# Four gated cross-attention layers: the stacks of score operands copied within SBUF, a shorter lead of the first pass, and the next layer's keys made during routing

## The chip, the core and the metric

The kernel runs on one core of a Trainium2 chip. A core has five engines with an instruction stream of their own: TensorE (PE; its weight loads are listed as PEld), VectorE (DVE), ScalarE (ACT), GpSimd (POOL) and SyncE (SP). They share SBUF (128 partitions) and pass matmul results through PSUM banks. Transfers between DRAM and SBUF, and within SBUF, are issued by an engine's queue and run on 16 DMA engines.

The metric is the device time of one execution in microseconds. Four runs of the kernel before gave 1860.47, 1851.73, 1857.73 and 1854.29 us, median 1856.01.

## The reference

There are 8 batch elements of 256 tokens and 256 features, a context of the same shape, and four layers. Each layer adds a gated cross-attention and a gated feed-forward part:

```python
x = x + tanh(g_xattn[l]) * xattn_l(layernorm(x), ctx)   # 16 heads of 16 features
x = x + tanh(g_ffn[l])   * ffn_l(layernorm(x))
# xattn: q = (x Wq + bq)/4, k = ctx Wk + bk, v = ctx Wv + bv;  softmax(q k^T) v Wo + bo
```

- Layer 0's attention has no projections (query and context are used as they are) and a mask over the keys. Its feed-forward part is a light and a heavy two-layer gelu network. All 256 tokens are routed to the heavy one.
- The feed-forward parts of layers 1 and 2 are mixtures of 8 experts. Each token takes the best two by its logits, weighted by a softmax over the two. The hidden widths are 1024 and 512.
- The feed-forward part of layer 3 quantizes activations and weights (to three values), convolves along the sequence over three tokens and applies silu.

## The kernel before

**Stages.** `attention(layers)` builds a region: (0, 1), then (2,), then (3,). The first region also carries layer 0's feed-forward part and the logits for layer 1's experts, the second the logits for layer 2's, the third the last feed-forward part (`pieces`). Between the regions stand `moe(...)`: `route` (best two experts), `slots` (a place for each token in 39 tiles of 128 rows, NTL = 39, by the matmuls rank L832 and tot L834 and a long row of VectorE operations behind them), and `experts`, which goes over the tiles: gather a tile's tokens, turn them (xgT L1000), hidden layer (hg L1020), output (ysb L1033), store to DRAM (yd L1034).

**A region's order.** `run` counts steps u, one per head and element (16 heads, so 128 steps per layer). At step u it emits `scores(u + LAG)` with LAG = 17, `probs(u)`, the values of an earlier head, and then whatever `plan` has put at that step. So the engines' order is written out by hand, and matmuls are pinned to it; other instructions may be moved by the scheduler within their dependences.

- `scores` makes the scores of one head (sc, L173) for its row maxima alone; VectorE reduces them (nm, L437, or with the mask ms, L432).
- `parts` and `rows` cut the negated maxima in three bf16 pieces, turn them and copy them (mt L463, then a DMA) into rows 112 to 114 of the query stack, once per half of an element (8 heads).
- `probs` makes the transposed scores again (st, L173), now with those three rows against rows of ones in the key stack, and ScalarE takes the exponential straight from PSUM (pT, L481).
- `values` multiplies by va, and `finish` projects and adds.

**The stacks.** Scores need more than one bf16 product. `split` cuts a float32 operand in three bf16 pieces with four operations (L182 to L185), and `stack` (from L240) puts pieces side by side along the contraction: seven groups of 16 partitions, the query's pieces in the order QP = (0, 1, 0, 1, 2, 0, 1), the key's in the order KP = (0, 1, 1, 0, 0, 2, 2). A stack has 16 partitions per group, and in each partition 8 heads x 512 columns. The source has its 128 partitions as (16 features, 8 heads), so partitions are regrouped on the way. Before, this goes over DRAM: one DMA writes the three pieces (dr, L248, 384 KB), then DMAs of whole rows of 8 KB read them back into the stack (L256), three for a query (neighbouring groups in one) and six for a key. SP issues them all. An element thus costs two splits, two writes and nine reads. The split of element 0 of a region runs on VectorE, the others on POOL.

```python
rows = dr.rearrange("i (d h) n -> (i d) (h n)", h=HC)
nc.sync.dma_start(st[k * DK : e * DK], rows[part[k] * DK : (part[e - 1] + 1) * DK])
```

The key stacks of elements 0 and 1 and of their values are kept outside the region (kkeep, vkeep, EARLY = 2). Their rows 96 and up are set to one by VectorE (L198).

**Preparation of an element** (`prep`): begin, `norm` (`stats` with the pow on POOL, L152, then xn L334, then x + gb on POOL, L339), `normT` (turn by TensorE, copy xs, L354/L356), `proj` of q (two halves oc = 0, 1: pq L173, then ScalarE's qT L375/L379), `proj` of k (kT L375/L381) and `vals` (va L393). Steps are counted from 16 (j - 2) - 3 for element j.

**What stands at a region's start.** Keys and values of elements 0 and 1 of the coming layer (`early`), with `setup` (weights and the product for gb), are made by `experts` at its last tiles: `setup` at tile 27, k and v of element 0 at tiles 32 to 35 and the others at the end. Before each element's norm the experts' results are added: `fetched` emits four gathers from yd on POOL (L950) at one step, `added` four VectorE operations (L1074) nine steps later. An element's first scores need its query stack, so at a region's start the chain is: gathers, added, statistics, pow, xn, turn, pq, qT, split, stack, score.

**The head.** The first region has x, context and mask loaded by SP (L281 to L285), the weights of the light and heavy network (L633 to L642) and the products with their gammas on POOL (L658, two of them on 128 x 1024).

Of the kernel before, what the change touches and what calls it, by code (L numbers as in the profile page):

```python
# [15 lines left out]
P = 128  # L16
# [12 lines left out]
LAG, AHEAD, VLAG = 17, 3, 1  # L29

# [6 lines left out]
def kernel(ctx: ExitStack, tc: tile.TileContext, a: dict, out: bass.AP):  # L37
# [51 lines left out]
    nc.vector.tensor_copy(identb, ident)  # L89
    nhalf = const.tile([P, 2, TPB], F32, tag="nhalf", name="nhalf")  # L90
# [44 lines left out]
    def stats(tiles, name, again=None):  # L135


        n = len(tiles)
        st = small.tile([P, TPB, 6], F32, tag="lnst", name=f"lnst_{name}")
        mv = small.tile([P, TPB, 2], F32, tag="lnmv", name=f"lnmv_{name}")  # L140
        for i, t in enumerate(tiles):
            nc.vector.bn_stats(st[:, i, :], x[t])
            nc.vector.bn_aggr(mv[:, i, :], st[:, i, :])
        k = 1 if again is None else 2
        ve = small.tile([P, 2, TPB], F32, tag="rsv", name=f"rsv_{name}")[:, :k, :n]
        nc.vector.tensor_scalar(ve[:, 0, :], mv[:, :n, 1], 1e-5, None, ALU.add)
        if again is not None:
            nc.vector.reciprocal(ve[:, 1, :], ve[:, 0, :])
            nc.vector.tensor_tensor(ve[:, 1, :], ve[:, 1, :], mv[:, :n, 1], ALU.mult)
            nc.vector.tensor_scalar(ve[:, 1, :], ve[:, 1, :], again[0], None, again[1])  # L150
        rs = small.tile([P, 2, TPB], F32, tag="rsr", name=f"rsr_{name}")[:, :k, :n]
        nc.gpsimd.tensor_tensor(rs, ve, nhalf[:, :k, :n], ALU.pow)  # L152
        return (mv, rs[:, 0, :]) if again is None else (mv, rs[:, 0, :], rs[:, 1, :])
# [42 lines left out]
    def ones_of(engine, va, ks=None):  # L196
        if ks is not None:
            engine.memset(ks[96:P], 1.0)  # L198
        engine.memset(va[:, :, :, DK : DK + 1], 1.0)
        engine.memset(va[:, :, :, DK + 1 :], 0.0)  # L200

    def attention(layers):
# [6 lines left out]
        stacks, vas = {}, []  # L209
# [28 lines left out]
        def stack(src, s, j):  # L238

            n = f"{s}{layers[0]}_{j}"  # L240
            pc = keep.tile([P, 3, DC * S], BF16, tag="pc", name=f"pc_{n}", bufs=2)
            r = keep.tile([P, DC * S], F32, tag="res", name=f"res_{n}")
            split(
                [pc[:, k] for k in range(3)], src.rearrange("p c s -> p (c s)"), r,
                nc.gpsimd if j and pool is not None else nc.vector,
            )
            dr = dram.tile([3, P, DC * S], BF16, tag=f"{s}dr", name=f"dr_{n}", bufs=2)
            nc.sync.dma_start(dr.rearrange("i p n -> p i n"), pc)  # L248
            st = stacks[s][j % 3].rearrange("r h c s -> r (h c s)")
            rows = dr.rearrange("i (d h) n -> (i d) (h n)", h=HC)  # L250
            part, k = QP if s == "q" else KP, 0
            while k < NS:
                e = k + 1
                while e < NS and part[e] == part[e - 1] + 1:
                    e += 1
                nc.sync.dma_start(  # L256
                    st[k * DK : e * DK], rows[part[k] * DK : (part[e - 1] + 1) * DK]
                )
                k = e
            return stacks[s][j % 3]  # L260

        ops = {}

        def prep(j, l, b):
# [4 lines left out]
            def begin():  # L269
                if l == 0 and j < EARLY:  # L270
                    ones_of(nc.vector, vas[j], stacks["k"][j])
                o["nm"] = pool.tile([P, 2, NH], F32, tag="nm", name=f"nm_{n}", bufs=3)

            def ones_own():

                nc.sync.dma_start(stacks["k"][j][NR : NR + 3], kkeep[0][NR : NR + 3])
                ones_of(nc.gpsimd, vas[j])

            def context():
                for i in range(2):  # L280
                    nc.sync.dma_start(x[2 * b + i], a["x"][b, i * P : (i + 1) * P, :])  # L281
                cx = pool.tile([P, 2, D], F32, tag="cx", name=f"cx_{n}", bufs=1)
                nc.sync.dma_start(cx, a["ctx_1024"][b].rearrange("(i p) d -> p i d", p=P))
                mk = pool.tile([P, 2, S], I32, tag="mk", name=f"mk_{n}", bufs=1)
                nc.sync.dma_start(  # L285
                    mk, a["mask_Bx1xSxS2_ik1"][b, 0].rearrange("(i p) k -> p i k", p=P)
                )
# [37 lines left out]

            def norm():
                xn = work.tile([P, 2, D], F32, tag="xn2", name=f"xn_{n}")
                mv, rs = stats([2 * b, 2 * b + 1], f"a{n}")
# [13 lines left out]
                o["xn"] = xn  # L342

            def normT():
# [10 lines left out]
                else:  # L355
                    nc.scalar.mul(xs, pt, 1.0 / DK**0.5)  # L356
                    o["qs"] = stack(xs, "q", j)
                o["xs"] = xs

            def proj(s, oc):  # L360
# [21 lines left out]
                if oc:  # L382
                    o[f"{s}s"] = stack(o["t"], s, j)
# [13 lines left out]
            own = [(0, ones_own)] if j == EARLY else []  # L397
            if l == 0:
                return own + [
                    (-3, begin), (-3, context), (-2, norm), (3, normT), (4, contextT), (5, biasT),  # L400
                    (6, contextV),
# [5 lines left out]
            if j < EARLY:  # L407
                early.extend([(NTL - 7 + i if j == 0 else NTL, f) for i, (_, f) in enumerate(kv)])
                kv = []
            return own + [  # L410
                (-6, begin), (-5, norm), (0, normT),
                (2, lambda: proj("q", 0)), (3, lambda: proj("q", 1)),
# [4 lines left out]
        def scores(u):  # L417
# [20 lines left out]
            if u - LAG in hold:  # L438
# [112 lines left out]

        def plan(at, f, *args):
            todo.setdefault(at, []).append(lambda: f(*args))

        for j, (l, b) in enumerate(jobs):
            if l and b == 0:
                if j:
                    plan(NH * (j - 2) - AHEAD - 6, setup, l)
                else:
                    early.append((NTL - 12, lambda l=l: setup(l)))  # L560
            for at, f in prep(j, l, b):
                plan(NH * (j - 2) - AHEAD + at, f)
            for c in range(DC):
                at = NH * j + HC * c + HC - LAG
                plan(at, parts, j, c)
                plan(at + 4, rows, j, c)
# [11 lines left out]
        def run(pool_, extra=(), ahead=()):  # L578
# [3 lines left out]
            for at, f in ahead:  # L582
                plan(at, f, pool)
                hold.add(at)
# [8 lines left out]
            for at, f in extra:  # L593
                plan(at, f)
            for u in range(min(todo), max(max(todo), NU + VLAG + 4) + 1):
                if 0 <= u + LAG < NU:
                    scores(u + LAG)
# [26 lines left out]
    def ffn0(pool):  # L624
# [5 lines left out]
        def load_weights():  # L630
            w1 = pool.tile([P, DC, NL + NHV], F32, tag="f0w1", name="f0w1", bufs=1)
            w2 = pool.tile([P, nh, D], F32, tag="f0w2", name="f0w2", bufs=1)
            nc.sync.dma_start(  # L633
                w1[:, :, :NL], a["L0_ffn_light_w1"].rearrange("(c p) h -> p c h", p=P)
            )
            nc.sync.dma_start(
                w1[:, :, NL:], a["L0_ffn_heavy_w1"].rearrange("(c p) h -> p c h", p=P)
            )
            nc.sync.dma_start(
                w2[:, 0:1, :], a["L0_ffn_light_w2"].rearrange("(c p) o -> p c o", p=P)  # L640
            )
            nc.sync.dma_start(  # L642
                w2[:, 1:, :], a["L0_ffn_heavy_w2"].rearrange("(c p) o -> p c o", p=P)
            )
# [11 lines left out]
            for c in range(DC):  # L656
                for cols, g in ((slice(0, NL), gl), (slice(NL, None), gh)):
                    nc.gpsimd.tensor_scalar(  # L658
                        w1[:, c, cols], w1[:, c, cols], g[:, c : c + 1], None, ALU.mult
                    )  # L660
            w.update(w1=w1, w2=w2, b1=b1, b2=b2[:, 0, :])
# [51 lines left out]
        return [(-LAG, load_weights)] + [q for b in range(B) for q in element(b)]  # L713
# [242 lines left out]
    def experts(l, pool, xd, chosen, rows, nh, scale, early, nsets, apart):  # L956
# [104 lines left out]
        def element(b):  # L1061
# [5 lines left out]
            def fetched(pool):  # L1067
                for k, (t, s, w) in enumerate(rows):
                    g.append(pool.tile([P, D], F32, tag="yg", name=f"yg{l}_{b}_{k}", bufs=4))
                    gather(g[k], yd[:, :], s[:, t : t + 1])  # L1070
# [8 lines left out]
            return [(at - 16, fetched), (at - 7, added)]  # L1079
# [212 lines left out]
    def moe(l, nh, nsets, apart, lg, xd, gate, early, scale=None):  # L1292
        with tc.tile_pool(name=f"c{l}", bufs=1) as pool:
            with tc.tile_pool(name=f"rt{l}", bufs=1) as tmp:
                chosen = route(pool, tmp, lg, gate, l)
                rows = slots(l, pool, tmp, chosen[0], chosen[1], nsets)
            with tc.tile_pool(name=f"f{l}", bufs=1) as tiles:
                return experts(l, tiles, xd, chosen, rows, nh, scale, early, nsets, apart)
# [13 lines left out]
    with tc.tile_pool(name="f3w", bufs=1) as home:  # L1312
        weights, pieces = ffn3(home)
        ahead = moe(2, 4, 5, False, lg[1], xd[1], tg[:, 6:7], early + weights, w["nw"])
# [90 lines left out]
```

## Time and profile before

The profile is of one execution of 1852.96 us; its span is 1851.2 us, with 27144 instructions. The runs' median is 1856.01 us.

| engine | busy us | share of the span |
|---|---|---|
| TensorE | 1430.1 | 77% |
| its weight loads | 1087.9 | 59% |
| VectorE | 926.5 | 50% |
| ScalarE | 740.2 | 40% |
| POOL | 676.0 | 37% |

The stages by the timeline of TensorE:

| from, to (us) | stage |
|---|---|
| 0 to 66.5 | head: loads, first norm, first stacks, scores up to the first st |
| 66.5 to 590 | region (0, 1) |
| 600 to 637 | routing and slots for layer 1's experts |
| 650 to 900 | layer 1's experts |
| 922 to 976 | start of region (2,) |
| 1201 to 1240 | routing and slots for layer 2's experts |
| 1250 to 1385 | layer 2's experts |
| 1390 to 1457 | start of region (3,) |
| 1457 to 1851 | region (3,) with the last feed-forward part |

How it is read: times are microseconds from the span's start. A line of a timeline has the start, the busy time, the engine, the line in the kernel, the operation, output<-inputs and how many such instructions are joined in it. In brackets stands the time in which the engine was idle before it and the work that ended this wait. "sc<-kstack,qstack" is the matmul that reads both stacks. The granted clock (PEclk) is a share of TensorE's full speed.

### The profile page before, as it was taken

How to read it: one execution, taken by the hardware profiler on the slowest of the kernel's cores; microseconds unless marked ns; L12 is line 12 of the kernel's file. 1: busy time of each engine (PE TensorE's matmuls, PEld its weight loads, DVE VectorE, ACT ScalarE, POOL GpSimd, SP SyncE). 2: the span in 40 equal slices, each digit the busy share in tenths (PEclk: the TensorE clock that was granted, in tenths of full speed). 3: DMA queues.
4: the chain of work that ended last, by engine and by line, in shares of the span. 5: the costliest groups of instructions: out<-in, count | busy, mean ns of one | idle time of the engine just before them, and what ended most of it. 6: DMA issues, size and time to landing. Idle time of an engine off the chain costs nothing. (4 is left out here: it accounts for less than half of the span.)

```text
span 1851.2 us, 27144 instructions
## 1 busy us (share of the span) xinstructions
PE 1430.1 (77%) x9856; PEld 1087.9 (59%) x9886; DVE 926.5 (50%) x2642; ACT 740.2 (40%) x1623; POOL 676.0 (37%) x807
## 2 busy tenths in 40 slices
PE   1598888989998499999947888739992676666653
PEld 1366566766665399999825565439991354444422
DVE  5655554445664411111154767453322657778777
ACT  0255444545554133333204555312330346455641
POOL 4342322332410344433154532025533435553452
PEclk9989999999998699999968999869996788888876
DMA  7653222223450423332454554153444434222000
GB/s 200 155 121 81 64 58 58 58 67 87 100 134 30 162 61 109 107 114 85 102 128 98 113 132 93 32 190 125 123 109 97 109 70 97 55 53 67 7 7 17
DMA packets 96381, 170.05 MB, mean 92 GB/s; under 512 B 26028, under 2 KB 80175, under 8 KB 85231
## 3 DMA queue, kind: packets, MB, share of 16 engines
q1 hardware_dynamic: 68114, 114.40, 25.1%
q0 software_dynamic: 23664, 52.81, 9.7%
q10 hardware_dynamic: 4470, 1.10, 0.3%
q8 instruction: 78, 1.28, 0.3%
q14 instruction: 55, 0.45, 0.1%
HBM read 224.69 MB, written 41.68 MB: 144 GB/s over the span
## 5 line engine op out<-in xcount | busy, mean ns | idle before, releaser
L481 ACT ACTIVATE pT<-st 128x512 f32<-128x512 f32 x512 | 298.3, 597 | 289.4 <-PE st L173 232.3
L437 DVE TENSOR_REDUCE nm<-sc 128x2 f32<-128x512 f32 x384 | 257.0, 684 | 150.2 <-PE sc L173 148.3
L173 PE MATMUL sc<-kstack,qstack 112*128 112x256 bf16 x1024 | 213.3, 294 | 119.1 <-DMA kstack<-dr_k 53.1
L1020 ACT ACTIVATE hg<-phg,we 128x128 f32<-128x128 f32 x468 | 133.8, 369 | 269.4 <-issue 232.5
L173 PE MATMUL phg<-xgT,we 128*128 128x128 f32 x1872 | 225.2, 277 | 9.3 <-DMA we<-in_L_ffn_w,sl_wrow 3.9
L173 PEld LDWEIGHTS phg<-xgT,we 128*128 128x128 f32 x1872 | 223.5, 194 | 14.8 <-issue 9.3
L173 PE MATMUL st<-qstack,kstack 115*128 115x256 bf16 x1024 | 206.2, 285 | 28.0 <-ACT pT L481 26.8
L173 PE MATMUL yg<-we,hg 128*128 128x256 f32 x936 | 214.6, 379 | 0.0
L173 PEld LDWEIGHTS <-qstack 112*128 112x128 bf16 x1024 | 100.7, 104 | 187.9 <-issue 109.4
L173 PEld LDWEIGHTS yg<-we,hg 128*128 128x128 f32 x936 | 171.9, 190 | 20.2
L173 PE MATMUL po<-pT,va 128*32 128x256 f32 x2048 | 149.9, 409 | 0.9
L432 DVE CUSTOM_DVE_ANT_0 ms<-sc,mb 128x256 f32<-128x256 f32 x256 | 107.6, 420 | 76.9 <-PE sc L173 66.7
L173 PEld LDWEIGHTS <-kstack 115*128 115x128 bf16 x1024 | 104.1, 102 | 55.2 <-issue 36.1
L1033 DVE TENSOR_TENSOR ysb<-yg,we 128x256 f32<-128x256 f32 x78 | 33.0, 424 | 165.2 <-PE yg L173 155.6
L950 POOL DMA_INDIRECT xg<-xd,sl_toki x78 | 76.9, 986 | 89.2 <-DVE sl_toki L946 65.9
L152 POOL TENSOR_TENSOR rsr_ff<-rsv_ff,nhalf 128x4 f32<-128x4 f32 (+2 forms) x24 | 24.4, 1017 | 226.3 <-DVE rsv_ff L150 120.3
L950 POOL DMA_INDIRECT yg<-yd,sl_si x64 | 62.6, 978 | 103.2 <-DVE x L1074 31.1
L173 PEld LDWEIGHTS po<-pT,va 128*32 128x32 f32 x2048 | 56.2, 114 | 60.8 <-issue 37.3
L1000 DVE COPY xgT<-ptg 128x256 f32<-128x256 f32 x39 | 16.6, 425 | 139.8 <-PE ptg L178 139.8
L178 PE MATMUL px<-ident,xn 128*128 128x128 f32 x128 | 26.9, 346 | 69.6 <-DVE xn L334 59.6
L182 POOL CAST pc_q<-qT 128x512 bf16<-128x512 f32 x22 | 13.8, 628 | 172.4 <-ACT qT L375 126.7
L173 PE MATMUL pq<-xs,wq 128*128 128x256 f32 x192 | 67.1, 483 | 4.4 <-ACT qT L375 1.9
(253 smaller groups left out, 2508.7 us busy)
## 6 DMA issues: line engine op xcount, KB each, us to landing
kstack<-dr_k SPq DMA_DIRECT2D x160, 128.0 KB
qstack<-dr_q SPq DMA_DIRECT2D x64, 256.0 KB
dr_q<-pc_q SPq DMA_DIRECT2D x32, 384.0 KB
dr_k<-pc_k SPq DMA_DIRECT2D x32, 384.0 KB
qstack<-dr_q SPq DMA_DIRECT2D x32, 384.0 KB
yd<-ysb SPq DMA_DIRECT2D x78, 128.0 KB
kstack<-dr_k SPq DMA_DIRECT2D x32, 256.0 KB
xd<-fxn_f SPq DMA_DIRECT2D x8, 512.0 KB
```

Source lines behind the costliest of these rows:

```text
L152: nc.gpsimd.tensor_tensor(rs, ve, nhalf[:, :k, :n], ALU.pow)
L173: pin(nc.tensor.matmul(out, lhsT=lhsT, rhs=rhs, start=start, stop=stop, skip_group_check=True))
L178: pin(nc.tensor.transpose(out, in_, idn))
L182: engine.tensor_copy(dst[0], src)
L432: nc.vector.tensor_tensor_reduce(masked, sc[:, i, :], o["bias"][:, i, :], -1.0, 3.0e38, ALU.add, ALU.min, o["nm"][:, i, h : h + 1],)
L437: nm = nc.vector.tensor_reduce(o["nm"][:, :, h], sc, AX.X, ALU.max, negate=True)
L481: pin(nc.scalar.activation(pT[u], st, AF.Exp))
L950: return nc.gpsimd.indirect_dma_start(out=dst, out_offset=None, in_=src, in_offset=bass.IndirectOffsetOnAxis(ap=rows, axis=0), **kw,)
L1000: nc.vector.tensor_copy(xT, pv)
L1020: nc.scalar.activation(h[:, hc, :], ph[:, k, :], AF.Gelu, bias=w[:, n1 - nh + hc : n1 - nh + hc + 1],)
L1033: nc.vector.tensor_tensor(ys, py, w[:, nh * D :], ALU.add)
```

## The change

1. `stack` has no way over DRAM any more. Seven DMAs of 16 partitions x 8 x 1 KB each copy a piece of the split result (pc, 128 partitions) straight into its group of the stack, ordered by piece, all on SP. 64 stacks: 448 such DMAs in place of 352.
2. In regions (2,) and (3,) element 0's query is stacked by halves: each `proj("q", oc)` is split at once (256 columns, VectorE) and copied into half c of the stack (rows of 512 B), its DMAs by turns on SP (4) and ACT (3). Element 1's query is split on VectorE, and key stacks always on POOL.
3. FIRST = 14: the first head is scored 14 steps ahead of its exponential. The lead grows by one head in two steps to 17 (`slot`). `parts` and `rows` of element 0 follow.
4. Element 1's preparation is planned 8 steps later. `stats` becomes a step of its own (`measure`), and in regions (2,) and (3,) its pow is pinned in program order for elements 0 and 1. The four gathers of an element are emitted one per step and pinned.
5. The ones rows of the key stack come by DMA from a tile of ones. The loads of the light and heavy network stand at step -4 and are pinned; the products with their gammas at steps 8 and 10, pinned on POOL. ctx is loaded ahead of x and mask in a pinned order.
6. `early` (setup, keys and values of elements 0 and 1) runs between `route` and `slots` and no longer in the last tiles of `experts`. The ternary weights of the last feed-forward part stay in `experts`.

The diff's core:

```diff
-LAG, AHEAD, VLAG = 17, 3, 1
+LAG, FIRST = 17, 14
+AHEAD, VLAG = 3, 1
...
-    def ones_of(engine, va, ks=None):
-        if ks is not None:
-            engine.memset(ks[96:P], 1.0)
+    def ones_of(engine, ks, va):
+        nc.sync.dma_start(
+            ks[NR : NR + 3].rearrange("r h c s -> r (h c s)"), onesb[: 3 * HC * DC * S // P]
+        )
...
-            dr = dram.tile([3, P, DC * S], BF16, tag=f"{s}dr", name=f"dr_{n}", bufs=2)
-            nc.sync.dma_start(dr.rearrange("i p n -> p i n"), pc)
...
+            if c is not None:
+                cols = slice(c * S, (c + 1) * S)
+                pc, r, src, st = pc[:, :, cols], r[:, cols], src[:, cols], st[:, :, c, :]
+            else:
+                st = st.rearrange("r h c s -> r h (c s)")
+            split([pc[:, k] for k in range(3)], src, r, engine or nc.gpsimd)
+            part = QP if s == "q" else KP
+            for n, (p, k) in enumerate(sorted((p, k) for k, p in enumerate(part))):
+                e = nc.scalar if c is not None and n % 2 else nc.sync
+                d = e.dma_start(st[k * DK : (k + 1) * DK], pc[:, p])
+                if layers[0] == 0 and j == 0:
+                    pin(d)
...
-                if oc:
-                    o[f"{s}s"] = stack(o["t"], s, j)
+                if s == "q" and lead and j == 0:
+                    o["qs"] = stack(o["t"], s, j, oc, nc.vector)
+                elif oc:
+                    o[f"{s}s"] = stack(
+                        o["t"], s, j, engine=nc.vector if s == "q" and lead and j == 1 else None
+                    )
...
             return own + [
-                (-6, begin), (-5, norm), (0, normT),
-                (2, lambda: proj("q", 0)), (3, lambda: proj("q", 1)),
+                (-6, begin), (-5, measure), (-3 + k, norm), (0 + k, normT),
+                (2 + k, lambda: proj("q", 0)), (3 + k, lambda: proj("q", 1)),
             ] + kv
...
+        slot = []
+        for u in range(-FIRST, NU):
+            while len(slot) < min(NU, u + 1 + min(LAG, FIRST + max(0, u // 2))):
+                slot.append(u)
...
             for c in range(DC):
-                at = NH * j + HC * c + HC - LAG
+                at = slot[NH * j + HC * c + HC - 1] + 1
                 plan(at, parts, j, c)
-                plan(at + 4, rows, j, c)
+                plan(at + (3 - (c == 0) if j == 0 else 4), rows, j, c)
...
-        return [(-LAG, load_weights)] + [q for b in range(B) for q in element(b)]
+        return [(-4, load_weights)] + [(8 + 2 * c, lambda c=c: gammas(c)) for c in range(DC)] + [
+            q for b in range(B) for q in element(b)
+        ]
...
-            return [(at - 16, fetched), (at - 7, added)]
+            return [(at - 16 + k, lambda p, k=k: fetched(p, k)) for k in range(4)] + [
+                (at - 7, added)
+            ]
...
                 chosen = route(pool, tmp, lg, gate, l)
+                for f in early:
+                    f()
                 rows = slots(l, pool, tmp, chosen[0], chosen[1], nsets)
```

In TensorE's order the early matmuls then stand behind plf (the logits of the last tokens) and ahead of tot: gb's product, k and v of element 0, k and half of v of element 1, rank, the rest of v, tot.

## The prediction

> **What bounds the kernel now.** I read the shares of the engines first.
>
> ```profile
> PE 1430.1 (77%) x9856; PEld 1087.9 (59%) x9886; DVE 926.5 (50%) x2642; ACT 740.2 (40%) x1623; POOL 676.0 (37%) x807
> ```
>
> TensorE leads, but 23% of the span it stands. Where it stands is told by windows cut at the stages' seams (the last column but two is the granted clock, then DMA share and GB/s):
>
> ```profile
> core 0: us, PE busy (x) PEld busy (x) DVE busy (x) ACT busy (x) POOL busy (x), PEclk, DMA share, GB/s
> 0.00:66.50 66.50, 14.24 (x62) 8.84 (x63) 39.07 (x133) 5.29 (x9) 25.58 (x40) 1.00 0.81 199
> 66.50:590.00 523.50, 471.25 (x3373) 333.39 (x3401) 277.49 (x1031) 273.08 (x510) 151.13 (x187) 0.96 0.34 81
> 600.00:637.00 37.00, 9.68 (x72) 8.82 (x73) 20.41 (x81) 1.82 (x4) 9.89 (x10) 0.53 0.26 97
> 650.00:900.00 250.00, 250.00 (x1715) 234.96 (x1714) 31.80 (x73) 79.05 (x276) 99.81 (x101) 1.00 0.34 103
> 922.00:976.00 54.00, 23.86 (x85) 14.41 (x84) 27.29 (x67) 5.19 (x13) 26.33 (x31) 0.66 0.49 115
> 1201.00:1240.00 39.00, 7.92 (x57) 6.85 (x56) 24.80 (x84) 0.49 (x2) 8.83 (x9) 0.51 0.38 132
> 1390.00:1456.70 66.70, 24.37 (x89) 14.72 (x88) 27.72 (x68) 5.84 (x13) 26.73 (x35) 0.62 0.41 95
> ...
> 1401.00:1403.00 2.00, 0.00 (x0) 0.00 (x0) 0.00 (x0) 0.00 (x0) 1.62 (x2) 0.50 1.01 135
> 949.50:952.50 3.00, 0.21 (x1) 0.24 (x2) 0.73 (x2) 0.00 (x0) 2.14 (x4) 0.50 1.02 254
> ```
>
> The first attention region is TensorE's (471 of 523), the experts wholly so (250 of 250). Between them lie five seams in which it idles: the head (to 66.5), two routings (600, 1201), the starts of the second and third region (922, 1390). The change works in all five. The timeline of TensorE names what ends a start's wait (in brackets: idle time before, and its releaser):
>
> ```profile
> 42.23 1.01 PE L173 MATMUL sc<-kstack,qstack 112*128 112x256 bf16 x4 [20.50 <-DMA kstack<-dr_k]
> 954.72 0.61 PE L173 MATMUL sc<-kstack,qstack 112*128 112x256 bf16 x2 [1.34 <-DMA qstack<-dr_q]
> 976.08 0.50 PE L173 MATMUL st<-qstack,kstack 115*128 115x256 bf16 x2
> 1001.61 0.58 PE L173 MATMUL sc<-kstack,qstack 112*128 112x256 bf16 x2 [6.29 <-DMA kstack<-dr_k]
> 1433.38 0.58 PE L173 MATMUL sc<-kstack,qstack 112*128 112x256 bf16 x2 [1.95 <-DMA qstack<-dr_q]
> ```
>
> The first scores (sc) wait for the stacks; a region's exponentials begin with st, 17 heads later. The chain into such a start is on the timelines of POOL and VectorE:
>
> ```profile
> 1399.80 0.97 POOL L950 DMA_INDIRECT yg<-yd,sl_si  x1 [24.65 <-DMA yd<-ysb]
> ...
> 1412.75 0.73 POOL L152 TENSOR_TENSOR rsr_a<-rsv_a,nhalf 128x2 f32<-128x2 f32 x1
> ```
> ```profile
> 943.03 0.43 DVE L182 CAST pc_q<-qT 128x512 bf16<-128x512 f32 x1 [6.37 <-ACT qT L379]
> ```
>
> **The stack's price.** No row shows an SBUF to SBUF stack. Both ends come from the two windows of 2 and 3 us above, in which the queues are full (share 1.0): reads into 16 partitions run at 135 GB/s, reads into 32 and 48 partitions at 254. One stack writes 7 x 128 KB = 0.92 MB: 6.8 us at 135; a 1 KB packet of the write to DRAM takes 46 ns in the DMA rows, and 56 such on each of 16 engines are 2.6 us. The new transfers have the k reads' target (16 partitions) but several are in flight, so I take 5 us and keep 2.6 and 6.8; plus some 2 us from issue to the first bytes, as before. What goes is the write of 384 KB and its wait: from the issue of the write (986.08) to the score (1001.61) are 15.5 us now, 7 then. SP issues 7 instead of 4 or 7 DMAs at about 0.4 us each, 2.8 us in a 27 to 48 us element period.
>
> The Trainium skill ("SBUF — State Buffer", Door 1: The DMA port swizzle) speaks against the change: 16 partitions reach 4 of 16 ports, measured there at 104 GB/s. The row has 135 for the same target. By 104 a stack would be 8.8 us, and the sum below worse by 3 starts x 1.5 stacks x 3.8 = 17 us.
>
> **Head: -17** (-10 to -20). The first score stands at 42.2 behind the k stack's reads, issued at 31.3. The diff takes two 3.47 us memsets of kstack off VectorE, the two 5.74 us gamma products off POOL ahead of the first pow, pins ctx and x in front of the other loads and drops the hop. What remains: statistics after small loads issued on ACT, about 14 to 16 (f0b is now earlier in VectorE's order, which is a new wait, and behind it stand the statistics); pow and xn to 20; four transposes, copy and split (0.4 + 0.7 + 0.4 + 0.7) to 24; transfer to 29. The k split moves from VectorE to POOL (0.61 + 1.16 + 0.61 + 1.16 = 3.5 us), beside the q chain. So the score comes 13 earlier. The second and third key waits (7.85 and 6.08 us of idle time before 65.7 and 90) shrink to about 1 each, one before and one after the first st; a lead of 14 heads saves three scores ahead of it, and they are paid back in the following 12 steps (+1.5). I take 17: 13 + 5 for the third key, less 1.5 (16.5).
>
> **Second region's start: -19** (-9 to -24). rsr is 2.05 us earlier, since the pow no longer stands behind element 1's gathers (0.97 + 0.30 us each, a row above shows them at the third region). Then halves: qT's first half is ready at 940.7, its second at 943.0 (ACT rows), so the split starts 2.3 earlier; four VectorE operations on 256 columns take about 1.3 in place of 2.24; the transfer is 0.46 MB, 1.3 to 3.4 us, plus 2, in place of the 9.3 from the write's issue (945.40) to the score at 954.72. Together the first score is at 943 to 945, 11 earlier. Three scores fewer ahead of st and rows at step -4: st at 961, 15 earlier. The third key's wait (6.29) falls to 1.3, and the lead's three heads are paid back with 1.2. -15 - 5 + 1.2 = -19. ACT issues three of each half's DMAs at 0.4 us: behind them on ACT stands qT's second half, 2.3 us later anyway.
>
> **Third region's start: -29** (-15 to -36). Here the key projections of the next layer were behind the last tile, so ysb on VectorE stood behind the k split (1393.4 to 1395.7) and the last expert output was stored late: yg's first gather on POOL at 1399.80. Without them -6.3. The 16-partition window at 1401 shows the k reads on full queues while the gathers ran; -4.2 for that collision. Pow -2.4 (it stands behind four gathers at 1412.75), halves -10.8, so the first score at 1409.7; st from 1456.7 to 1429.5, 27 earlier; third key -5, lead +2: -30, of which I take 29.
>
> **Routing: +7.7 and +4** (4 to 15, 0 to 12). The keys and values of elements 0 and 1 (eight groups of 1.03 us at full clock, the gb product 0.5) now stand in TensorE's program order behind plf and before tot. plf ends at 600.2, rank starts at 604.79 after 4.60 us of idle time: at full clock that gives tot's end at 600.2 + 8.7 + 1.4 = 610.3 in place of 606.0, +4.3; the groups share two PSUM banks and each waits for ACT's copy of an earlier one, eight at 0.4, so 3.3 more: +7.7 for tot, and for sl_c and every gather of the experts behind it. In the second routing two sums over weights (2.29 us each, L1114) now fall into that wait: +4. The granted clock of this window was 0.53, so the groups may take twice as long: with that it is 4.3 + 8.7, and 2 for the copies: +15. Four casts of kT and va on ACT (0.4 us each, ACT busy 1.8 of 37) and the k splits on POOL (3.5 each, POOL 9.9 of 37) are hidden by idle engines; if slots' own POOL work queues behind them, up to 3.5 us more, inside the bound.
>
> The sum takes full clock, since between 938.8 and 942.2 TensorE was about 86% busy and full clock followed. The Trainium skill ("TensorE: Matmul & The Clock Gate", Part 1) starts a burst at half clock until a window of about 3.4 us has been busy; by it the groups would cost 1.7 more in each routing.
>
> **Experts: -4.6 and -5.6.** The same projections leave a stage in which TensorE is 100% busy: four groups on the path at 1.03 plus the gb product 0.5 in the first, five in the second; the remaining groups stood behind the last tile, in the idle time of the start.
>
> **Sum:** -17 + 7.7 - 4.6 - 19 + 4 - 5.6 - 29 = -63.5 on the profiled execution of 1852.96: 1789.5. The median of the runs is 3 above that execution, so 1792 (the rivals' times have these 3 too). Steady state costs nothing: DMA share is 0.34 and 0.22 there, TensorE covers it.
>
> **Rivals.**
> (A) The transfers are bound at the target's partitions, each hop saved is partly paid again: at 6.8 us and more the starts give -8, -11 and -22, the rest as above: 1816. For it: 135 GB/s; against: 46 ns packets.
> (B) Routing on half clock and a POOL queue: +15 and +12 in place of 7.7 and 4: 1808. For it the 0.53; against, eight groups in a row are themselves a busy window.
> (C) Slower: packets of 1 KB from 128 source partitions are so slow that the stacks set the element's period. Each element needs 14 transfers of 128 KB, t us each. The periods are 34 and 31 us (first region), 27 (second), 48 (third), so t = 1.93 fills the second region. Each us of t above 1 costs the three starts 31 us (3.5 for a half, 7 for a key stack). At t = 2.15 the gain is used up; at 2.4 it is 43 + 8 x 6.6 + 8 x 2.6 = 117 against 63.5: 1909. For it: many small packets; against: the k reads move 128 KB in 0.97 us.
> (D) The starts come earlier, but the region behind is held by something of its own (third region: VectorE 288 of 394) and takes the time back: 1856.
>
> **Chances.** Forecast 0.52, A 0.20, B 0.14, C 0.10, D 0.04. Faster by over 0.3% (5.6 us, about what a measurement can tell) is forecast, A and B: 0.86; D is same, 0.04; C slower, 0.10. The predicted time is the forecast's. Its bounds at the good end (-20, +4, -24, 0, -36, and -10 for the experts) sum to -86, 1770, and I take 1766, since a stack of 2.6 us is only partly in them; at the high end the starts give only their least (-10 - 9 - 15) with both routings at their worst, -17: 1839.
>
> **What would show it.** Right: sc first at 29, near 943 and 1410; st first at 52, 961, 1430 less the shift of what came before (seams compared from the end of the stage before); no kstack wait over 2 us; tot some 8 us later than plf; the experts 5 us shorter. Wrong: kstack waits that grow, DMA share at 1 in the regions, an ACT row behind its own DMA issues, or xn waiting on pow. The prediction fails if a stack takes over 10 us from split to score.

## The result and the profile after

The changed kernel takes 1858.13 us (median of 52 runs, 1850.22 to 1866.08); the kernel before, over 78 runs, 1854.38. The ratio is 1.0018, 95% interval 1.0010 to 1.0026: no gain where 64 us were forecast. The changed profile is of a span of 1854.7 us.

First the page's engine line, then the windows of the changed kernel, cut at the same seams as before (first score pass to the first st, region (0, 1), routing, start of region (2,), second routing, start of region (3,)):

```profile
PE 1450.9 (78%) x9856; PEld 1099.8 (59%) x9886; DVE 916.4 (49%) x2641; ACT 741.5 (40%) x1623; POOL 682.0 (37%) x815
```
```profile
0.00:56.70 56.70, 12.47 (x57) 8.15 (x58) 28.18 (x115) 5.30 (x9) 15.36 (x35) 0.93 0.69 102
56.70:605.70 549.00, 477.99 (x3347) 336.90 (x3377) 282.54 (x1043) 271.66 (x506) 159.31 (x192) 0.93 0.43 67
606.00:661.40 55.40, 26.12 (x133) 17.89 (x133) 28.44 (x97) 6.61 (x16) 13.85 (x15) 0.71 0.42 74
...
947.40:994.00 46.60, 19.06 (x65) 11.77 (x65) 26.65 (x65) 4.20 (x10) 22.59 (x26) 0.60 0.46 86
1226.30:1269.40 43.10, 17.75 (x76) 11.93 (x76) 25.60 (x84) 3.61 (x9) 12.93 (x14) 0.62 0.63 131
1419.80:1466.50 46.70, 18.11 (x65) 11.37 (x66) 27.18 (x65) 5.05 (x10) 22.72 (x30) 0.63 0.48 85
```

The seams are shorter (head 56.7 in place of 66.5, start of region (3,) 46.7 in place of 66.4), but region (0, 1) is 549 us long from its first st to its last, 518 before. Its DMA share rose from 0.34 to 0.43 while the GB/s fell from 81 to 67: fewer bytes took longer.

The timelines of before and of the changed kernel, subtracted stage by stage (the marks are the first st, the end of plf, the first phg, the end of the last expert output yg, and the last matmul), give where the time went. The last three columns are experiments told below.

| stage, us against before | predicted | changed | e1 | e7 | e8 |
|---|---|---|---|---|---|
| head, to the first st | -14.5 | -9.9 | -6.3 | -19.2 | -7.7 |
| region (0, 1), to the end of plf | -2.5 | +30.0 | +2.5 | -4.1 | +3.3 |
| routing 1 | +7.7 | +9.6 | +9.2 | +9.2 | 0.0 |
| experts 1 | -4.6 | -4.0 | -4.1 | -4.1 | -4.3 |
| start of region (2,), to its first st | -15 | -7.7 | -8.5 | -8.8 | -7.3 |
| region (2,) | -4 | +7.2 | -6.5 | -11.8 | -11.6 |
| routing 2 | +4 | +8.0 | +8.1 | +8.0 | +0.4 |
| experts 2 | -5.6 | -3.7 | -4.2 | -2.6 | -0.9 |
| start of region (3,), to its first st | -27 | -19.7 | -20.2 | -20.1 | -19.7 |
| region (3,) | -2 | -5.8 | -14.7 | -12.7 | -10.7 |
| sum | -63.5 | +4.0 | -44.7 | -66.2 | -58.5 |

What the extra time of the regions waits for, on the timeline of TensorE in the changed kernel:

```profile
34.36 2.16 PE L177 MATMUL sc<-kstack,qstack 112*128 112x256 bf16 x8 [18.14 <-DMA kstack<-pc_k]
...
56.66 0.58 PE L177 MATMUL st<-qstack,kstack 115*128 115x256 bf16 x2 [3.52 <-DMA qstack<-mt]
...
64.50 1.01 PE L177 MATMUL sc<-kstack,qstack 112*128 112x256 bf16 x4 [3.84 <-DMA f0w<-in_L_ffn_light_w]
...
93.39 0.58 PE L177 MATMUL sc<-kstack,qstack 112*128 112x256 bf16 x2 [6.86 <-DMA kstack<-pc_k]
...
512.57 0.49 PE L177 MATMUL sc<-kstack,qstack 112*128 112x256 bf16 x2 [3.04 <-DMA kstack<-pc_k]
```

The first score is at 34.36, not at 29, though the normalized element is turned at 13.8 and SP issues the stacks from 16. The key stacks still end waits (62.6 us of idle time over 13 waits in the whole trace, 53.1 over 9 before), and a wait that was not there stands before st: mt, the row maxima, whose small DMA lands late (47.7 us over 21 waits of TensorE and its weight loads). The window in which only two stacks are under way shows their rate:

```profile
20.00:30.00 10.00, 0.00 (x0) 0.00 (x0) 0.00 (x0) 0.00 (x0) 1.37 (x2) 1.00 1.16 114
```

All queues full (share over 1) and 114 GB/s. The records of the DMA engines have about 111 packets of 1 KB a us there, some 163 ns each; a stack of 896 packets takes 8.1 us and its key stack stands behind it. The same in a steady stretch (463 to 468 us): 113 GB/s.

The rate is not all. SP's own waits show that it often stands before the issue of a stack's DMA until a DMA of mt has landed; before the change no stack waited so. In the trace each of these issues waits for the very semaphore that it will signal itself, and that an mt DMA, issued by ACT, signalled last; the kernel's text does not choose these semaphores. First the sum of these waits (us, times, longest), then one of them:

```profile
SPq L265 <- DMA qstack<-mt: 185.9, 37, 9.2
...
1157.00:1163.00 6.00, 6.00 (x59) 3.76 (x58) 4.53 (x11) 3.30 (x8) 0.00 (x0) 1.00 0.27 35
1161.73 0.75 ACTq L482 DMA_DIRECT2D qstack<-mt  x1
1163.95 0.55 SPq L265 DMA_DIRECT2D kstack<-pc_k  x1
1167.12 0.38 PE L177 MATMUL sc<-kstack,qstack 112*128 112x256 bf16 x2 [3.56 <-DMA kstack<-pc_k]
```

Six of this key stack's DMAs are issued by 1154.8. The seventh waits for mt until 1163.95, with the queues at 0.27 from 1157 to 1163, and the score waits for the seventh. In 10 of the 13 waits for a key stack (33.9 of the 62.6 us) the stack's last DMA had waited like this, for 3.5 to 9.2 us.

### The profile page after: what moved, and what is told of

It reads as the page before. It is cut to its first block, busy times and chain, and to the rows that moved or that the text cites. A ratio compares the mean times of both kernels' runs of the same rounds, so it can differ in the third digit from the quotient of the medians.

```text
span 1854.7 us, 27500 instructions
## 1 busy us (share of the span) xinstructions
PE 1450.9 (78%) x9856; PEld 1099.8 (59%) x9886; DVE 916.4 (49%) x2641; ACT 741.5 (40%) x1623; POOL 682.0 (37%) x815
## 4 chain that ended last, share of the span: by engine, by line
PE 57%; DVE 16%; DMA 12%; issue 6%; POOL 5%; ACT 3%; SPq 1%; ACTq 0%; POOLq 0%; DVEq 0%
PE yg L177 11%; PE phg L177 11%; DMA qstack<-mt 5%; PE po L177 4%; PE y_f L177 4%; PE st L177 4%; PE sc L177 4%; PE ph_f L177 4%; DMA kstack<-pc_k 3%; PE pk L177 3%; PE pq L177 3%; PE pv L177 2%; DVE nm L455 2%; DVE ms L450 1%; PE py L177 1%
## 5 line engine op out<-in xcount | busy, mean ns | idle before, releaser
L177 PE MATMUL sc<-kstack,qstack 112*128 112x256 bf16 x1024 | 216.6, 301 | 119.7 <-DMA kstack<-pc_k 62.6
L177 PE MATMUL st<-qstack,kstack 115*128 115x256 bf16 x1024 | 213.0, 293 | 48.8 <-DMA qstack<-mt 23.5
L177 PEld LDWEIGHTS yg<-we,hg 128*128 128x128 f32 x936 | 171.9, 190 | 20.2
L177 PEld LDWEIGHTS po<-pT,va 128*32 128x32 f32 x2048 | 56.7, 115 | 62.7 <-issue 39.3
L177 PE MATMUL pq<-xs,wq 128*128 128x256 f32 x192 | 73.2, 519 | 3.8 <-ACT qT L384 1.5
L177 PE MATMUL ph_f<-xT_f,f0w 128*128 128x256 f32 x288 | 68.2, 394 | 3.8 <-DVE nm L455 2.1
L1253 POOL TENSOR_TENSOR h_f<-h_f,z_f 128x512 f32<-128x512 f32 x28 | 36.6, 1305 | 85.4 <-ACT pT L499 35.4
```

The source lines that it names most:

```text
L177: pin(nc.tensor.matmul(out, lhsT=lhsT, rhs=rhs, start=start, stop=stop, skip_group_check=True))
L1253: nc.gpsimd.tensor_tensor(y, y, z, ALU.add)
```

## The experiments

Each ran beside the kernel before on the same chip; times are medians.

### The transfer alone, out and in (e1, e2)

e1 is the changed kernel with the DRAM way put back, for halves too:

```diff
-            for n, (p, k) in enumerate(sorted((p, k) for k, p in enumerate(part))):
-                d = e.dma_start(st[k * DK : (k + 1) * DK], pc[:, p])
+            nc.sync.dma_start(dr.rearrange("i p n -> p i n"), pc)
+            rows = dr.rearrange("i (d h) n -> (i d) h n", h=HC)
+            ...   # the reads of before, three for q, six for k
```

> The changed kernel with the stacks filled over DRAM again (part 1 undone, parts 2 to 6 kept; halves go over DRAM too). Theory T: a 1 KB packet from SBUF into 16 partitions takes about 160 ns on every DMA engine (113 packets a us in the changed kernel's head), so a stack holds the queues 7.9 us and the loads, row pieces and key stacks behind it come late; that made region (0, 1) 31 us longer (first st to last st 549 us, 518 before). T expects 518 to 527 us there and a total of 1830 to 1845. Rival R: the 31 us come from the schedule (lead of 14, element 1 eight steps later, loads and gammas moved). R expects 540 us or more there and a total of 1855 or more.

Measured: 1809.17 us, ratio 0.9766 (0.9739 to 0.9794). First to last st of region (0, 1): 520.4 us. The region is where T expected it, and R falls; the total is 21 us below T's range. SP waits for mt before a stack only once here (4.0 us). The share of the DMA engines from the first st to the end of plf is 0.37, against 0.43 in the changed kernel: the way over DRAM keeps the engines almost as busy, but key stacks end only 5 waits, of 28.8 us, in place of 13 of 62.6.

e2 is the kernel before with the seven DMAs in place of the ten.

> The kernel before with part 1 alone (seven SBUF to SBUF DMAs per stack, all on SP). T expects region (0, 1) longer by 10 to 30 us (first st to last st 528 to 548) and a total of 1865 to 1885. R expects every stage within 3 us of before and a total within 5 us of 1855.

Measured: 1877.69, ratio 1.0128 (1.0100 to 1.0155); region (0, 1) 534 us, region (2,) 12 us longer. Part 1 alone costs 24 us, and taken out of the change it gives 49. Why it costs twice as much beside the other parts is not shown. SP's waits for mt are here too: 196.8 us in 38 waits. R falls.

### Is it the 16 partitions? (e7, e10, e11)

e7 keeps bytes, packets and SBUF to SBUF, and spreads the target: eight DMAs into 112 partitions, of one head each, in place of seven into 16.

```diff
-                d = e.dma_start(st[k * DK : (k + 1) * DK], pc[:, p])
+                d = e.dma_start(stacks[s][j % 3][:NR, n], pc[:NR, n % 3])   # n = 0..7
```

> The changed kernel with the same bytes and packets of 1 KB (896 a stack, halves of 512 B) moved from SBUF to SBUF, but each of eight DMAs spread over 112 target partitions in place of seven into 16. The scores are then of wrong rows; all the work is done. Theory T (the 16 target partitions are what makes a packet take 160 ns): packets near 50 ns, a stack in about 3 us, region (0, 1) from first to last st 510 to 522 us (549.0 in the changed kernel), total 1795 to 1820. Rival S (an SBUF to SBUF packet is slow by itself, or the number of DMAs): packets stay over 120 ns and the total at 1850 or more.

Measured: 1786.17, ratio 0.9635 (0.9619 to 0.9651). First score at 24.1, first st at 47.3, region (0, 1) 514.8 us, packets of 54 to 56 ns in every stretch. The experts take 285.8 us here and 286.0 in the changed kernel, so other data did not change their work. Its window:

```profile
20.00:30.00 10.00, 4.14 (x14) 1.34 (x13) 3.89 (x18) 0.00 (x0) 1.14 (x2) 1.00 0.66 190
```

190 GB/s with the engines two thirds busy, and TensorE already scores. S falls: an SBUF to SBUF packet isn't slow by itself. The total is 9 us below T's range, and more than the rate has changed. Each of e7's DMAs holds one head, so a head can be scored when its own rows have landed: the first score starts before SP has issued all eight DMAs of the key stack.

```profile
21.67 5.05 SPq L267 DMA_DIRECT2D kstack<-pc_k  x8
24.07 3.23 PE L177 MATMUL sc<-kstack,qstack 112*128 112x256 bf16 x10 [8.26 <-DMA kstack<-pc_k]
```

Each row also stays in its own partition, and no issue of a stack waits for mt. So e7 shows the rate of the packets, but not that the rate alone is worth the 72 us.

e10 goes half way: 32 partitions with half the heads in each of six DMAs (the first four heads need four of the seven).

> The changed kernel with six of a stack's seven DMAs into 32 partitions with half the heads each, the seventh into 16, bytes and packets the same; the scores are then of wrong rows, all the work is done. If the time of a packet goes with the number of target partitions (160 ns into 16, 55 into 112), it is 80 to 100 ns here and the total between e7's 1786 and the changed kernel's 1858: 1800 to 1825. If more than 16 partitions is enough, near 55 ns and 1786 to 1795.

Measured, one run, so without an interval: 1783.66. Its window from 20 to 30:

```profile
20.00:30.00 10.00, 0.00 (x0) 0.00 (x0) 0.00 (x0) 0.00 (x0) 1.21 (x2) 1.00 1.16 137
```

Full queues, 137 GB/s, so 20% more than into 16, and 134 ns a packet against 163; over 130 to 440 us, full queues or not, a packet takes 82 ns on average, against 119 in the changed kernel and 55 in e7. The packet lies between, as the first theory expected; the total does not, it is e7's. So the time does not go with the packet. The waits of TensorE in region (0, 1), from its first to its last st, are shorter, first the changed kernel, then e10 (sum, times, longest), with SP's waits for mt behind:

```profile
PE sc L177 <- DMA kstack<-pc_k: 17.2, 4, 6.9
PE st L177 <- DMA qstack<-mt: 8.9, 3, 3.6
PE sc L177 <- DMA f0w<-in_L_ffn_light_w: 3.8, 1, 3.8
```
```profile
PE st L177 <- DMA qstack<-mt: 4.7, 2, 3.2
PE sc L177 <- DMA kstack<-pc_k: 3.3, 1, 3.3
...
PE sc L177 <- DMA f0w<-in_L_ffn_light_w: 1.1, 1, 1.1
...
SPq L269 <- DMA qstack<-mt: 8.8, 4, 4.7
```

17.2 + 8.9 + 3.8 = 29.9 us of DMA waits against 9.1: 20.8 of the 34.9 us by which this stretch is shorter. Three things differ from the changed kernel: packets (134 ns for 163), the heads that a score, or the refilling of a stack, has to wait for, and SP's waits for mt (8.8 us for 185.9). Which of them brings the time back is open: no run changes one without the others, and the changed kernel with a semaphore of its own for mt was not run. (The wait put down to f0w is of element 1's first score; the scores read no f0w, so the releaser named there can't be the cause. Element 1's key stack, issued just ahead of f0w, is what they read; its third DMA waited 6.2 us for mt.)

e11 asks whether two queues help: `e = nc.scalar if n % 2 else nc.sync` for every stack.

> The changed kernel with every stack's seven DMAs issued by turns on SP (4) and ACT (3), as it does for the halves alone. Theory T: two queues in flight write two groups at once, of which most pairs have no partitions in common, so packets fall from 160 to 80 to 120 ns, the key stacks land in time, and the total is 1790 to 1825. Rival Q: the DMA engines are shared, packets stay near 150 ns, and ACT's issues (0.6 to 0.7 us, three a stack, ahead of its exponentials) cost more: 1855 or more.

Measured: 2006.20, ratio 1.0812 (1.0776 to 1.0848). From 20 to 30 us packets take 164 ns (113 GB/s), as in the changed kernel; Q holds for the rate, and T falls. Its price is larger than an issue: a DMA on ACT waits for its split, and ScalarE's exponentials stand behind it. On ScalarE's timeline, and in its waits (pT is the exponential; the two sums are 147 us, and the changed kernel's exponentials have no such wait):

```profile
225.50 3.38 ACTq L265 DMA_DIRECT2D qstack<-pc_q  x3
228.91 1.28 ACT L723 ACT_TABLE_LOAD   x1 [4.12 <-POOL pc_q L189]
...
ACT pT L499 <- POOL pc_k L189: 87.0, 19, 5.9
...
ACT pT L499 <- POOL pc_q L189: 60.1, 14, 7.3
```

### Reading back faster (e4, e5)

e4 changes the order of the groups so that DRAM is read in three DMAs per stack, a query's by repeating a piece: `rows[n : n + 1].to_broadcast([m, DK, HC, w])`. It also moves the early keys (as e3).

> e1 and e3 together, with the groups reordered (QP 0,0,0,1,1,1,2 and KP 0,1,2,0,1,2,0) so that each stack is read back from DRAM by three DMAs into 48, 48 and 16 partitions. T and P expect their gains to add, and a key stack 3 us sooner than in e1: a total of 1805 to 1825. If reads into 48 partitions are no quicker than into 16 beside other work, the total is e1 plus e3's gain alone, 1815 to 1830; under R it is 1838 or more.

Measured: 1996.02, ratio 1.0771 (1.0738 to 1.0804). A window of its head shows what went wrong:

```profile
30.00:36.00 6.00, 0.00 (x0) 0.00 (x0) 0.00 (x0) 0.00 (x0) 0.00 (x0) 1.00 0.19 70
```

The share is 0.19 at 70 GB/s. That fits 3 of 16 engines (0.1875), and the outermost dimension of these DMAs is 3 long; which engines ran is not shown. So e4 tells nothing of wider targets; it is most likely a mistake of shape. e5 keeps whole rows as the outermost dimension, with QP = (0, 1, 0, 1, 0, 1, 2) and KP = (0, 1, 2, 0, 1, 2, 0).

> e1 (stacks over DRAM) with the seven groups in another order, QP 0,1,0,1,0,1,2 and KP 0,1,2,0,1,2,0, so that a key stack is read back by three DMAs (48, 48, 16 partitions) in place of six, a query stack by three as before. T: reads into 48 partitions run at 254 GB/s against 135, so a key stack comes 2 to 3 us sooner where the first pass waits for it (third key of three regions): 1798 to 1807 after e1's 1809. If the reads hide behind other work there, 1807 to 1811.

Measured: 1809.44, ratio 0.9758 (0.9733 to 0.9782), the same as e1. The reads were hardly sooner: between 130 and 590 us a key stack's packets of 8 KB take 4.7 to 5.5 us from the first to the last, in e1 about 6.0, while a query's take 5 in place of 4.2. So e5 does not tell whether sooner reads would hide. A stack in 5 us is some 180 GB/s, not 254; the window of 3 us in which 254 was read holds gathers of POOL too.

### The keys during routing (e3, e6, e8)

In the changed kernel the groups stand between plf and tot:

```profile
621.39 2.08 PE L177 MATMUL pk<-ctxT,wk 128*128 128x256 f32 x4
...
625.85 1.91 PE L177 MATMUL pv<-wv,ctxT 128*128 128x256 f32 x4
...
629.44 1.03 PE L177 MATMUL pk<-ctxT,wk 128*128 128x256 f32 x4
...
635.05 0.49 PE L865 MATMUL tot<-sl_both,ones 128*128 128x128 f32 x2 [0.46 <-ACT va L407]
```

The first groups take 2.08 us, at half clock (PEclk 0.50 from 621.39 to 625), the later ones 1.03 (1.00 from 629.4 to 635); tot starts 14.7 us after plf, 5.2 before. The forecast had full clock. e3 puts the groups behind tot, where TensorE waits for VectorE:

```diff
-                for f in early:
-                    f()
-                rows = slots(l, pool, tmp, chosen[0], chosen[1], nsets)
+                rows = slots(l, pool, tmp, chosen[0], chosen[1], nsets, early)
...
+        pin(rank), pin(tot) in banks of ps_t and ps_s
+        for f in early:
+            f()
```

> The changed kernel with the early keys and values behind rank and tot in TensorE's order, rank, tot and tok in other PSUM banks. Theory P: the eight groups ahead of tot cost 9.8 and 11.8 us on the path (tot after plf's end: 14.7 and 16.6 us, 4.9 before), and behind tot they fall into TensorE's wait for VectorE. P expects tot 5 us after plf, the first expert matmul 8 to 12 us earlier in each routing and a total of 1836 to 1844. Rival: the groups take another place on the path (tok waits behind them, or POOL's key splits come ahead of the gathers), total 1850 or more.

Measured: 1854.33, ratio 1.0007 (0.9991 to 1.0022), by the medians some 4 us less than the changed kernel, by the ratios 2; P expected 14 to 22. tot came 9.5 us nearer to plf, as expected, and the first phg only 4.1: the rival. VectorE's row behind tot had become longer, for instance:

```profile
634.93 1.76 DVE L955 TENSOR_TENSOR sl_aa<-iot,sl_jj 128x624 f32<-128x624 f32 x1
...
637.34 1.13 DVE L918 CAST sl_wrow<-sl_wr 128x39 int32<-128x39 f32 x1
```

The same two take 0.80 and 0.18 us in the changed kernel. POOL's key splits ran beside them, and they too were longer (the first cast 2.73 us, 0.61 in the changed kernel). In e6, with no split on POOL there, sl_aa takes 0.80 us again, so the two engines held each other up here. The later runs take the splits off POOL: e6 has the projections behind tot and the two key splits as VectorE work planned at the experts' third and sixth tile, on e5.

> e5 with the early keys and values behind rank and tot in TensorE's order and the splits of these two key stacks on VectorE at the third and sixth tile of the experts. In e3 tot came 9.7 us earlier and the first expert matmul only 4.4: VectorE's row behind tot took longer beside POOL's splits (sl_aa 1.76 us in place of 0.81, sl_wrow 1.13 for 0.18, the cast on POOL 2.73 for 0.61). Theory: without POOL's splits there the whole 9 and 8 us come back: 15 to 18 us less than e5. Rival: the groups themselves delay tok or the gathers: 8 us less than e5 or fewer.

Measured: 1811.74, ratio 0.9791 (0.9756 to 0.9826), with four runs between 1805.89 and 1823.54: no gain that can be told. The splits were still moved ahead: nothing held them in their tile, they ran before sl_toki, and their stacks' transfers were in front of the experts' first gathers. On TensorE:

```profile
626.00 0.66 PE L182 MATMUL ptg<-ident,xg 128*128 128x128 f32 x2 [11.22 <-DMA xg<-xd,sl_toki]
633.57 6.68 PE L177 MATMUL phg<-xgT,we 128*128 128x128 f32 x32 [6.90 <-DMA we<-in_L_ffn_wa,sl_wrow]
```

e8 pins the splits and xgT on VectorE.

> e6 with the two key splits and xgT pinned on VectorE, so that the splits really stand at the third and sixth tile (in e6 they were still moved ahead of sl_toki, their stacks' transfers went in front of the experts' first gathers, and xg came 9.4 us after its index where it takes 4.2 before). Theory: with the splits and their transfers in the experts, the first expert matmul follows plf by 31 us as before (40.5 in the changed kernel, 42.4 in e6) and the groups' 9 and 8 us come back: 1793 to 1800. Rival: the transfers then delay the experts' weight gathers by as much: 1805 to 1812.

Measured: 1793.88, ratio 0.9666 (0.9650 to 0.9683): 3.3% faster than the kernel before, and the best that computes the whole. The same place:

```profile
600.97 0.63 PE L888 MATMUL tot<-sl_both,ones 128*128 128x128 f32 x2
...
623.12 0.66 PE L182 MATMUL ptg<-ident,xg 128*128 128x128 f32 x2 [4.76 <-DMA xg<-xd,sl_toki]
627.38 5.54 PE L177 MATMUL phg<-xgT,we 128*128 128x128 f32 x32 [3.60 <-DMA we<-in_L_ffn_wa,sl_wrow]
```

The first phg comes 31.6 us after plf, as before the change: the groups now cost the routing nothing.

### The first element's stacks, and the lead (e9, e12)

e9 is e8 with element 0's stacks by SBUF to SBUF.

> e8 with element 0's stacks (the two halves of the query, in the first region query and key) copied from SBUF to SBUF as in the changed kernel, all others over DRAM. In the changed kernel the first score came 1.6 to 4.1 us earlier after its stage's start than in e1 (head 34.4 against 38.4). Expected: 4 to 8 us less than e8, 1787 to 1796. Rival: the slow packets in front of the next loads give it back: within 3 us of e8.

Measured: 1804.44, ratio 0.9727 (0.9711 to 0.9743), 10.6 us more than e8; both expectations missed. The first score came 2.3 us earlier, the first st 3.5, but the first score of element 1 waited 10.21 us where e8's waits 1.47:

```profile
52.76 0.72 SPq L700 DMA_DIRECT2D f0w<-in_L_ffn_heavy_w  x1
...
55.48 1.53 SPq L286 DMA_DIRECT2D kstack<-dr_k  x3
...
69.52 1.01 PE L177 MATMUL sc<-kstack,qstack 112*128 112x256 bf16 x4 [10.21 <-DMA kstack<-dr_k]
```

It isn't the slow packets that stand in front: SP issued element 0's stacks by 26, and the queues were empty at 43. It is the loads of layer 0's feed-forward weights (f0w), which SP issues from 44.05 to 53.48 here, between element 0's stacks and element 1's reads, and from 23.98 to 32.21 in e8. Why they come later here is not shown, so e9 does not price the direct copy of one element.

e12 is e8 with `FIRST = 17`.

> e8 with the first pass 17 heads ahead again (FIRST = 17). The prediction gave the lead of 14 about 2 us at each of three starts, of which 1 to 2 are paid back. In the runs the time from the first score to the first st hardly moved between before (24.3, 21.4, 23.3 us) and e8 (22.4, 20.9, 20.0). Expected if the lead is worth what the prediction said: 1794 to 1799; if element 1's work on VectorE fills the time anyway: within 2 us of e8's 1794.

Measured: 1811.89, ratio 0.9772 (0.9744 to 0.9799), 18.0 us more than e8; both missed. The first st of the three regions came 15.0, 4.0 and 5.1 us later after the first score. In the head:

```profile
53.53 0.38 PE L177 MATMUL sc<-kstack,qstack 112*128 112x256 bf16 x2 [0.67 <-DVE nm L473]
73.26 1.01 PE L177 MATMUL sc<-kstack,qstack 112*128 112x256 bf16 x4 [19.36 <-DMA x<-in_x]
74.07 0.63 PE L177 MATMUL st<-qstack,kstack 115*128 115x256 bf16 x2
```

With a lead of 17 the scores ahead of the first st include head 16, which is element 1's first. It needs element 1's stacks, and with its preparation eight steps later they come late; the first st stands behind it. (As above, the releaser is one whose tile the scores don't read.)

## Why the prediction was wrong

**The step that failed** is "The stack's price" with its conclusion in "Sum": "I take 5 us and keep 2.6 and 6.8", and "Steady state costs nothing: DMA share is 0.34 and 0.22 there, TensorE covers it". A stack takes 8.1 us, outside both ends: the 135 GB/s of the upper end was of 8 KB rows, and 1 KB packets into the same 16 partitions run at 114. And the price falls due for every element, not at three starts. Regions (0, 1) and (2,) got 30.0 and 7.2 us longer where 2.5 and 4 less were forecast; with the stacks over DRAM again (e1) they are at +2.5 and -6.5, so the direct copies are what costs there. A query and a key stack take 16 us of full queues in an element of 27 to 34, and the share of the DMA engines, averaged over a region, does not show that the key stack behind them is late for its first score. The prediction also counted only SP's time to issue, not what an issue can wait for: 185.9 us for mt. The key stack of the score at 1167.12 was issued from 1149.8 on, which is over the 10 us from split to score that the prediction set as its limit. How much of the loss is the slow packets and how much these waits stays open.

**The rest of the sum** came out near in e7, -66.2 us of the span's stages against -63.5, 1786.17 us against 1792. That is in part luck. The terms missed in both directions: the head gave 19.2 there in place of 14.5 (with scores that start on part of a stack), the second region's start 8.8 in place of 15, the third's 20.1 in place of 27, region (2,) 11.8 in place of 4, region (3,) 12.7 in place of 2.

**Rival A** had the mechanism, targets that bound the transfer, and the lower bound of its price, but sized it at the starts alone: 1816. **Rival C** named the other half, stacks that set the element's period, from a t of 1.93 us. Measured t is 8.1/7 = 1.15. Its threshold was computed as if only the queues' total time counted; the loss began long before, since a stack has a due time within the period. **Rival D** has the nearest number, 1856, by luck: it saw region (3,) take the time back, which got 5.8 us shorter; the time was lost in the other two, by the stacks.

**Routing** was forecast +7.7 and +4, measured +9.6 and +8.0, in between the forecast and rival B. The reason for taking full clock, a window at 938.8, did not carry over: here the first three groups and most of the fourth ran at half clock. The Trainium skill ("TensorE: Matmul & The Clock Gate", Part 1), set aside in the prediction, has a burst begin so, which these rows show, though for some 8 us and not 3.4. The second routing did hide the two sums (3.6 us, as 4 was forecast), but tot came 11.6 later there.

**The rule set aside at the stack** (the Trainium skill, "SBUF — State Buffer", Door 1: The DMA port swizzle) has 104 GB/s for 16 partitions and 189 for 32. The runs show 114 and 137 here, the first near it, the second not; and its 8.8 us a stack was nearer to the measured 8.1 than the 5 taken. That two queues at once are no quicker (e11) is not explained by the runs.

**The lead of 14** was priced at three scores, about 2 us less 1 to 2 paid back, a start. e12 shows 18 us in all, with element 1's preparation eight steps later than before, for a reason the prediction did not name though its profile had the wait (7.85 us before 65.7): head 16 is another element's.

**The halves** gave less than forecast: from the turn to the first score of region (2,) it takes 12.1 us, 18.3 before and some 10 by the forecast's times, and the lead's gain to the first st was eaten by element 1's query split and additions on VectorE, in front of the reductions: from the first score to st are 22.0 us, 21.4 before.

## What to carry to other kernels

Cost a DMA by its target partitions and its packet together, and count it for every iteration, with the time at which its consumer needs it: an average share of the queues hides a transfer that is late each time. Look at what the issuing queue waits for, too: an issue can stand behind the landing of another engine's small DMA. When a hop over DRAM is removed, compare the rate of the direct copy, not the number of hops. Work moved into a stage that "waits" needs three looks: at the engine it waits for, at engines that slow each other, and at the queue in front of the next transfer; and a pin, or the scheduler puts it elsewhere.

## What the runs showed of the hardware that was not expected

- SBUF to SBUF packets of 1 KB took 163 ns into 16 partitions with full queues, 134 into 32 and 56 into 112, there each in its own partition and with the engines two thirds busy (114, 137 and 190 GB/s); a second issuing queue changed nothing (164 ns, e11).
- In the changed kernel SP stood 185.9 us, in 37 waits, before the issue of a stack's DMA until a small DMA of another engine's queue, which signals the same semaphore, had landed; 4.0 in one wait with the stacks over DRAM (e1).
- With DMAs whose outermost dimension was 3 the share of the DMA engines was 0.19 (e4).
- Instructions of VectorE and POOL that ran side by side in e3 took longer: 1.76 us for 0.80, 2.73 for 0.61.
